# Reordering the first and the last steps of an attention stage: k's products first, first u's squares early, a copy of u later

## The chip, the cores and the metric

The kernel runs on one core of one Trainium2 chip. The metric is the device time of one execution in microseconds (us). It has five engines that matter here: TensorE (PE) for products, VectorE (DVE) and ScalarE (ACT) for element-wise work and for emptying PSUM, GpSimd (POOL) for small sums, and SyncE (SP), which only issues DMA transfers. ACT issues some transfers too. Each engine works through its own instructions in order and waits for the others by semaphores.

## The reference

The input x has 2 sequences of 2048 rows of 256 numbers, all in 32-bit floats. Four parts are added to x in turn, each on layer-normalised rows:

```python
x = x + attn_a(layernorm(x))   # gated scan: q * scan(a, kv)
x = x + ffn(layernorm(x))      # 256 -> 1024 -> 256, ternary weights, gelu
x = x + attn_b(layernorm(x))   # 16 heads of 64, below
x = x + ffn(layernorm(x))      # the same weights again
```

The third is the part that the change touches. With q, k and v from x by three 256 x 1024 matrices, each head carries three 64 x 64 states through time, and the result goes through W_o:

```python
k_C = k_t @ C_QV                  # then, per head:
G    = G    + outer(k_t, k_C)
S_K  = S_K  + outer(k_t, k_t)
C_QV = C_QV + outer(q_t, v_t)
o_t  = q_t @ (S_K @ C_QV - G)
```

## The kernel before

The program has three stages. The first does the gated scan and the first ffn (to about 310 us), the second the attention with states (310 to about 1040 us, overlapped with the first block of the last ffn), the third the rest of the last ffn.

The attention works in chunks of 128 rows. There are 32 steps `s`; step `s` is chunk `n = s // 2` of sequence `s % 2`, so that an even step (`first`) and the odd step after it form a pair. The states are rewritten as running sums: u is q times the running sum S of k's outer products, with a masked part inside the chunk, and o is q times the running sum M of outer products of u and v, built in the same way. The helpers for a step are these:

- `Seven` (L732) makes one of q, k, v for the two chunks of a pair with seven products instead of eight. `go` (L784) takes their numbers. Product 2 goes to bank Y and 1 to bank X; 0 stands for the addition of Y by DVE; 5 goes to bank Z; 6 and 7 go on top of X, 3 on top of Z, 4 on top of X again. Products 1, 5, 6 and 4 are followed by a copy out of their bank by ACT (L791, L796, L799, L808), products 7 and 3 by an addition on DVE (L782). Since 6, 7 and 4 write on the bank that the step before still has to be read from, each waits for the copy or the addition ahead of it. The tag (`uT`, `oT`) says from which two of the PSUM banks X and Z come; Y comes from a ring of four.
- `keys_out` (L946) and `units_out` (L949) turn a chunk of k or u into the other layout: DVE transposes squares of 32 x 32 (L923), SP writes them to DRAM (L925). `turn_rows` (L928) reads them back with four gathers on SP's queue (L933) into one of two buffers `raw`. `turn_end` (L939) and `units_end` (L952) copy the result on ACT (L943, to kT or uN).
- `inter` (L839) and `intra` (L855) make u or o from the state and from within the chunk, `products` (L823) the masked products q by k or q by u (DVE applies the mask at L837), `evict` (L869) empties the two banks of u or o in three copies (L873, L875), `update` (L878) adds to a state: S from k and k, M from u (uN) and v.
- `units` (L956) is the last step's way to uN: PE transposes and DVE copies (L818).
- `Last` (L1139) works the first block of the last ffn into the last steps: `part` issues blocks of 256 KB of its weights on ACT's DMA queue (L348), `begin` and `fill` (L1186, L1194) do its products (hx, hy, hz at L394).

The order of the work on PE, DVE, ACT and POOL is written by hand: it is the order of the calls. SP's transfers follow the same order. L964 to L985 open the stage, before the loop over the steps; the loop is L986 to L1109. What matters in it: at L1012 an even step copies the last step's u (`units_end(s - 1)`) ahead of its own work inside the chunk, and so does the last pair's odd step; the other odd steps do it at L1043, behind the evictions. An even step puts its own u out only at L1077 and reads it back at L1096.

Of the kernel before, what the change touches and what calls it, by code (L numbers as in the profile page):

```python
# [43 lines left out]
def kernel(  # L44
# [662 lines left out]
    def attention(keep, pool, state, last):  # L707
# [161 lines left out]
        def evict(s, nm, copy=act):  # L869
            b, n = steps[s]  # L870
            banks = d[s][nm + "b"]
            t = pool.tile([P, NPR, P], FP, tag=nm, bufs=2 if nm == "uT" else 1, name=f"{nm}{b}_{n}")
            copy(t[:, :, halves[0]], banks[0])  # L873
            for h in range(2):
                copy(t[halves[h], :, halves[1]], banks[1][halves[h ^ 1], :, :])  # L875
            d[s][nm] = t

        def update(s, left, right, sums):  # L878


            b, n = steps[s]
            prev = before.get((b, sums))
            last = n == CPB - 1
            banks = [bank([P, NPR, DK], f"h{sums}{b}_{n}_{c}") for c in range(1 if last else 2)]
            for p in range(NPR):
                for c in range(len(banks)):
                    for h in range(2):
                        nc.tensor.matmul(  # L888
                            banks[c][halves[h], p, :], lhsT=d[s][left][halves[c], feats(h, p)],
                            rhs=d[s][right][halves[c], feats(h, p)], start=True, stop=True,  # L890
                        )
            d[s][sums] = [prev]
            for c in range(len(banks)):
                t = state.tile([P, NPR, DK], FP, tag=f"{sums}{b}", bufs=3, name=f"{sums}{b}_{n}_{c}")
                if prev is None:
                    nc.vector.tensor_copy(t, banks[c])
                else:
                    nc.vector.tensor_tensor(t, prev, banks[c], ALU.add)  # L898
                d[s][sums].append(t)
                prev = t  # L900
            before[b, sums] = prev
# [26 lines left out]
        def turn_rows(s, nm):  # L928

            b, n = steps[s]  # L930
            raw = pool.tile([P, P, NPR], FP, tag="raw", bufs=2, name=f"r{nm}{b}_{n}")
            for b_ in range(NQ):
                nc.sync.dma_start(  # L933
                    out=raw[b_ * SQ : (b_ + 1) * SQ].rearrange("i (a j) q -> i a (j q)", a=NQ),
                    in_=d[s]["d" + nm][:, :, b_, :].rearrange("a i c -> i a c"),
                )
            d[s]["r" + nm] = raw

        def turn_end(s, nm):  # L939

            b, n = steps[s]
            t = pool.tile([P, NPR, P], FP, tag=nm, bufs=1, name=f"{nm}{b}_{n}")
            act(t, d[s]["r" + nm].rearrange("p t q -> p q t"))  # L943
            d[s][nm] = t

        def keys_out(s):  # L946
            turn_squares(s, "kT", d[s]["kN"].rearrange("t (q b i) -> t b q i", q=NPR, b=NQ))
# [8 lines left out]
        def units(s):  # L956
            uT = d[s]["uT"]
            turned(lambda p: uT[:, p, :], s, "uN", "raw")
            d[s]["uN"] = d[s]["uN"].rearrange("p a e -> p (a e)")
# [4 lines left out]
        NS = len(steps)  # L964
        pair_sums(0)
        stats = norm_stats(norm_pool, pair(1), bias=True)
        k, q = Seven(0, "kN", "uT"), Seven(0, "qT", "oT")
        k.go(2, 1)
        q.go(2, 1)
        k.go(0, 5, 6)  # L970
        q.go(0, 5, 6)
        xn = norm_rows(norm_pool, pair(1), stats)
        k.go(7, 3)
        keys_out(0)
        turn_rows(0, "kT")
        q.go(7)
        k.go(4)
        q.go(3, 4)
        v = Seven(0, "vN", "oT")
        v.go(2, 1)  # L980
        v.go(0, 5, 6)
        update(0, "kN", "kN", "S")
        v.go(7, 3)
        keys_out(1)
        turn_end(0, "kT")  # L985
        for s in range(NS):  # L986
            first, n = s % 2 == 0, s // 2
            more = n + 1 < CPB
            inter(s, "S", "uT")
            products(s, "kT", "p1")  # L990
            if first and n + 2 < CPB:
                stats = norm_stats(norm_pool, pair(n + 2), bias=True)
            elif s == NS - 4:
                last.stats()
            elif s == NS - 2:
                last.second_stats()
            if s == 0:
                v.go(4)
                pairs[1] = norm_turned(norm_pool, pair(1), xn, bufs=1)
                pair_sums(1)  # L1000
            if s % 2 == 1 and more:
                q, v = Seven(n + 1, "qT", "uT"), Seven(n + 1, "vN", "oT")
            if s == 1:
                q.go(2)
                v.go(2)
                keys_out(s + 1)
            elif s % 2 == 1 and s + 1 < NS:
                keys_out(s + 1)
            if s == 2:
                k = Seven(n + 1, "kN", "uT")  # L1010
                k.go(2)
            if s > 0 and (first or not more):  # L1012
                units_end(s - 1)
            last.part()
            if s >= 3:
                outward(s - 3, 1)
            intra(s, "S", "kN", "p1", "uT")
            if s >= 2:
                intra(s - 2, "M", "vN", "p2", "oT")
            if s + 1 < NS:  # L1020
                turn_rows(s + 1, "kT")
            evict(s, "uT")
            if not more:
                if s >= 2:
                    evict(s - 2, "oT")
                last.begin(first)
                fill = last.fill
                fill(2)
                if not first:
                    units(s)  # L1030
                fill(2)
            elif first:
                if s != 2:
                    k = Seven(n + 1, "kN", "uT")
                    k.go(2)
                k.go(1)
                if s >= 2:
                    evict(s - 2, "oT")
                k.go(0, 5)
            else:  # L1040
                if s >= 2:
                    evict(s - 2, "oT", dve)
                units_end(s - 1)  # L1043
                units_out(s)
                turn_rows(s, "uN")
                if s > 1:
                    q.go(2)
                    v.go(2)
                q.go(1)
                v.go(1)  # L1050
                q.go(0, 5)
                v.go(0, 5)
                q.go(6)
                v.go(6)
            last.part()
            if s == NS - 1:
                last.second_rows()
            if s + 1 < NS:
                update(s + 1, "kN", "kN", "S")
            if s >= 1:  # L1060
                update(s - 1, "uN", "vN", "M")
            if s == NS - 1:
                update(s, "uN", "vN", "M")
            if first and not more:
                turn_end(s + 1, "kT")
            if not more:
                fill(2)
            elif first:
                k.go(6, 3, 7)
            else:  # L1070
                v.go(7)
                q.go(7)
                v.go(3, 4)
                q.go(3)
            last.part()
            if first:
                units_out(s)  # L1077
            if more:
                turn_end(s + 1, "kT")
            if s >= 1:  # L1080
                inter(s - 1, "M", "oT")
                products(s - 1, "uT", "p2")
            if not more:
                fill(1)
            elif first:
                k.go(4)
                if n + 2 < CPB:
                    xn = norm_rows(norm_pool, pair(n + 2), stats)
                else:
                    last.rows()  # L1090
            else:
                q.go(4)
            if not first and s + 2 < NS:
                keys_out(s + 2)
            if first:
                turn_rows(s, "uN")  # L1096
            if not first and n + 2 < CPB:
                pairs[n + 2] = norm_turned(norm_pool, pair(n + 2), xn, bufs=1)
                pair_sums(n + 2)
            elif s == NS - 3:  # L1100
                last.turned()
            if s == NS - 4:
                last.weights(True)
            elif s == NS - 3:
                last.part(None)
                last.weights(False)
            last.part()
            if s >= 2:
                outward(s - 2, 0)  # L1109
# [17 lines left out]
    def pair(n):  # L1127
        return [b * CPB + n for b in range(B)]
# [96 lines left out]
    with tc.tile_pool(name="keep", bufs=3) as keep_pool:  # L1225
# [10 lines left out]
        with tc.tile_pool(name="ffn2", bufs=1) as ffn_pool, tc.manual_schedule(engines=by_hand):  # L1236
            tags = ("uT", "ps", "oT")
            steps = last.outs
            for i, g0 in enumerate(blocks):
                more = i + 1 < len(blocks)  # L1240
# [57 lines left out]
```

## Time and profile before

| | us |
|---|---|
| three runs, median (lowest to highest) | 1240.7 (1238.59 to 1245.66) |
| profiled execution, whole | 1239.59 |
| profiled execution, span | 1237.8 |
| PE busy | 1217.9 (98%) |
| DVE busy | 753.2 (61%) |
| ACT busy | 588.0 (48%) |
| PE busy in 350 to 360 us | 4.91 of 10 |
| PE busy in 500 to 900 us | 399.17 of 400 |
| PE busy in 1000 to 1020 us | 17.17 of 20 |
| mean granted PE clock | 0.999 |

The span runs from the first to the last instruction of the profiled execution; its whole time is 1.8 us more. A line of a profile names the engine, the line of the kernel, the tile written and the tiles read (hqT_X is bank X of q's products, hkN of k's, hvN of v's; huT, hoT, hS, hM and hp are the banks of u, o, S, M and the masked products), the shape and the count. In a list of waits it says who waited for whom, the total, the times and the longest.

### The profile page before, as it was taken

What the parts mean: (1) busy time and instruction counts of PE and PEld (TensorE: products, weight loads), DVE (VectorE), ACT (ScalarE), POOL (GpSimd) and SP (SyncE); (2) the same over time, 40 slices, a digit from 0 to 9 for tenths busy, and PEclk for the clock granted to TensorE, in tenths of its full rate; (3) what the DMA queues carried; (4) which work ended last, traced back from release to release, by engine and by line L of the source; (5) the groups of instructions that cost most, each with busy time, mean ns of one, the idle gap of its engine ahead of it and who ended that gap; (6) DMA issues with size and microseconds to landing.
All of it is one profiled execution on the core that took longest, in us unless ns stands there. A gap on an engine that the chain in (4) does not pass through costs nothing.

```text
span 1237.8 us, 46471 instructions
## 1 busy us (share of the span) xinstructions
PE 1217.9 (98%) x21244; PEld 976.1 (79%) x21244; DVE 753.2 (61%) x1261; ACT 588.0 (48%) x960; POOL 217.9 (18%) x363
## 2 busy tenths in 40 slices
PE   9999999999989999999999999999999989999998
PEld 7588777999557787777777778777777879999998
DVE  7965664665456565566557666665666644566654
ACT  4355544543445445444454544545454553445442
POOL 3743143322101100110110010011011100322230
PEclk9999999999999999999999999999999999999999
DMA  9210000000232233233233223323322530000001
GB/s 325 105 60 1 1 1 1 1 2 1 70 104 89 88 122 108 69 116 111 76 101 105 97 86 122 106 81 105 105 93 83 177 110 11 30 22 18 18 18 34
DMA packets 60995, 91.98 MB, mean 74 GB/s; under 512 B 6112, under 2 KB 49376, under 8 KB 60544
## 3 DMA queue, kind: packets, MB, share of 16 engines
q1 hardware_dynamic: 58272, 84.96, 20.4%
q10 hardware_dynamic: 2448, 3.93, 1.1%
q8 instruction: 166, 2.72, 0.9%
q0 software_dynamic: 80, 0.14, 0.1%
q14 instruction: 29, 0.24, 0.1%
HBM read 48.11 MB, written 40.89 MB: 72 GB/s over the span
## 4 chain that ended last, share of the span: by engine, by line
PE 95%; DMA 2%; DVE 1%; ACT 1%; issue 1%; SPq 0%; POOL 0%; ACTq 0%; DVEq 0%; POOLq 0%
PE ox L485 9%; PE hy L909 9%; PE hx L394 9%; PE pq L272 6%; PE hkN_X L777 5%; PE hqT_X L772 5%; PE hp L831 5%; PE oz L485 5%; PE hvN_X L777 4%; PE hz L394 4%; PE hoT L848 3%; PE hS L888 3%; PE huT L862 3%; PE huT L848 3%; PE hM L888 2%; PE hoT L862 2%
## 5 line engine op out<-in xcount | busy, mean ns | idle before, releaser
L837 DVE TENSOR_TENSOR p<-hp,mask 128x512 f32<-128x512 f32 x128 | 82.1, 683 | 99.2 <-PE hp L831 99.2
L909 PE MATMUL hy<-wo,oT 128*128 128x256 f32 x512 | 123.6, 385 | 0.0
L909 PEld LDWEIGHTS hy<-wo,oT 128*128 128x128 f32 x512 | 93.6, 190 | 18.9 <-issue 6.7
L729 POOL TENSOR_TENSOR S<-xnT 128x128 f32<-128x128 f32 x32 | 14.8, 461 | 527.4 <-ACT xnT L205 509.7
L406 ACT ACTIVATE hT<-hT,b_sb 128x256 f32<-128x256 f32 x192 | 85.4, 500 | 32.8 <-DVE hT L438 31.3
L272 PE MATMUL pq<-xnT,wqkva 128*128 128x512 f32 (+1 forms) x216 | 84.8, 547 | 0.3 <-ACT xnT L216 0.3
L873 ACT COPY uT<-huT 128x512 f32<-128x512 f32 x32 | 18.8, 586 | 136.8 <-PE huT L862 136.8
L898 DVE TENSOR_TENSOR S<-S,hS 128x512 f32<-128x512 f32 x60 | 41.3, 688 | 58.9 <-PE hS L888 55.4
L188 ACT ACTIVATE xn<-x_sb,nb,rs 128x256 f32<-128x256 f32 x124 | 64.7, 592 | 16.4 <-POOL nb L174 16.4
L943 ACT COPY uN<-ruN 128x1024 f32<-128x1024 f32 x31 | 64.4, 2078 | 14.1 <-DMA ruN<-duN 12.5
L272 PEld LDWEIGHTS pq<-xnT,wqkva 128*128 128x128 f32 x216 | 40.0, 190 | 37.3 <-issue 34.7
L943 ACT COPY kT<-rkT 128x1024 f32<-128x1024 f32 x32 | 66.6, 2081 | 2.6 <-DMA rkT<-dkT 2.6
L923 DVE STREAM_TRANSPOSE skT<-kN 128x1024 f32<-128x1024 f32 x32 | 65.6, 2050 | 0.0
L491 DVE TENSOR_TENSOR x_sb<-x_sb,ox 128x256 f32<-128x256 f32 x64 | 26.8, 418 | 63.0 <-PE ox L485 63.0
L923 DVE STREAM_TRANSPOSE suN<-uT 128x1024 f32<-128x1024 f32 x31 | 63.6, 2050 | 2.0 <-ACT uT L875 1.6
L412 ACT COPY hT<-hx 128x512 f32<-128x512 f32 x32 | 18.8, 586 | 91.3 <-PE hx L394 91.2
L156 DVE BATCH_NORM_STATS2 st<-x_sb 128x6 f32<-128x256 f32 x128 | 51.4, 402 | 2.9 <-DMA x_sb<-in_x_dram 2.4
L888 PEld LDWEIGHTS hS<-kN 64*64 64x64 f32 x1984 | 32.8, 134 | 24.2 <-issue 24.2
L371 POOL TENSOR_TENSOR xT<-xnT 128x256 f32<-128x256 f32 x15 | 10.9, 727 | 223.7 <-ACT xnT L218 223.7
L808 ACT COPY vN<-hvN_X 128x512 f32<-128x512 f32 x16 | 9.4, 587 | 80.0 <-PE hvN_X L777 80.0
L782 DVE TENSOR_TENSOR kN<-kN,hkN_Y 128x512 f32<-128x512 f32 x16 | 11.0, 688 | 57.0 <-ACT kN L791 57.0
L218 ACT COPY xnT<-pt 128x512 f32<-128x512 f32 x32 | 17.2, 589 | 58.5 <-PE pt L212 50.7
(243 smaller groups left out, 2915.0 us busy)
## 6 DMA issues: line engine op xcount, KB each, us to landing
dkT<-skT SPq DMA_DIRECT2D x32, 512.0 KB, 3.3
rkT<-dkT SPq DMA_DIRECT2D x128, 128.0 KB, 2.9
duN<-suN SPq DMA_DIRECT2D x31, 512.0 KB, 3.4
ruN<-duN SPq DMA_DIRECT2D x124, 128.0 KB, 3.1
out_dram<-x_sb SPq DMA_DIRECT2D x16, 256.0 KB, 2.1
x_sb<-in_x_dram SPq DMA_DIRECT2D x7, 512.0 KB, 8.9
dw<-w SPq DMA_DIRECT2D x2, 1024.0 KB, 3.9
w_back<-dw ACTq DMA_DIRECT2D x8, 256.0 KB, 4.5
```

The lines of the kernel that those rows point to most:

```text
L188: nc.scalar.activation(xn[:, c, :], x_sb[:, g, :], AF.Identity, bias=nb[:, c : c + 1], scale=rs[:, c : c + 1],)
L272: nc.tensor.matmul(pq[:, :nt], lhsT=wqkva[:, d, col : col + P], rhs=xnT[:, d, :], start=(d == 0), stop=(d == ND - 1),)
L394: nc.tensor.matmul(at[a][:, j, :], lhsT=A[:, f * P : (f + 1) * P], rhs=Bm, start=(new and j == 0), stop=True, skip_group_check=True,)
L406: nc.scalar.activation(out, out if src is None else src[:, j, :], AF.Gelu, bias=b1_sb[:, f : f + 1])
L485: nc.tensor.matmul(banks[name][:, c, :], lhsT=A[f // 2][:, f % 2, c * P : (c + 1) * P], rhs=Bm[:, f, :], start=(new and c == 0 and f == 0) ...
L777: nc.tensor.matmul(to, lhsT=self.A[i], rhs=self.B[i], start=new, stop=True, skip_group_check=True)
L837: nc.vector.tensor_tensor(d[s][nm][:, h], banks[h], mask8, ALU.mult)
L848: nc.tensor.matmul(banks[c][halves[h ^ c], p, :], lhsT=d[s][sums][c][halves[h], p, :], rhs=d[s]["qT"][halves[h], p, halves[c]], start=(p = ...
L888: nc.tensor.matmul(banks[c][halves[h], p, :], lhsT=d[s][left][halves[c], feats(h, p)], rhs=d[s][right][halves[c], feats(h, p)], start=True ...
L909: nc.tensor.matmul(py, lhsT=d[s]["oT"][:, p, :], rhs=wo[:, p, :], start=(p == 0), stop=(p == NPR - 1),)
L923: nc.vector.transpose(sq.rearrange("p b j q -> p b q j"), src)
L943: act(t, d[s]["r" + nm].rearrange("p t q -> p q t"))
```

## The change

Four things are done; the arithmetic stays the same.

1. At the opening of the stage k takes its banks from `oT` and q from `uT` (before the other way round). k's products come earlier than before among q's, and v's first ones are mixed in among the last ones of k and q. `keys_out(0)` with its gathers follows k's product 3, `keys_out(1)` k's product 4; before, the second stood at the end of the opening. v's product 6 now comes after `update`, right ahead of 7, and `turn_end(0)` moves ahead of v's 7 and 3.
2. In step 0, u goes out and is read back as soon as it is evicted (`units_out`, `turn_rows` behind k's product 1) instead of at the end of the step, and k's products 6, 3, 7 become 6, 7, 3.
3. In step 1, the copy of step 0's u moves from before step 1's own squares to behind the products 6 of q and v.
4. In the last step (31), the copy of step 30's u moves from before the work inside the chunk to behind the first two ffn products (the `fill(2)` at L1028), just ahead of `units`.

```diff
@@ -964,25 +964,29 @@
         NS = len(steps)
         pair_sums(0)
         stats = norm_stats(norm_pool, pair(1), bias=True)
-        k, q = Seven(0, "kN", "uT"), Seven(0, "qT", "oT")
-        k.go(2, 1)
-        q.go(2, 1)
-        k.go(0, 5, 6)
+        k, q, v = Seven(0, "kN", "oT"), Seven(0, "qT", "uT"), Seven(0, "vN", "oT")
+        k.go(2, 1, 0, 5)
+        q.go(2)
+        k.go(6)
+        q.go(1)
+        k.go(3)
+        keys_out(0)
+        turn_rows(0, "kT")
+        k.go(7)
         q.go(0, 5, 6)
         xn = norm_rows(norm_pool, pair(1), stats)
-        k.go(7, 3)
-        keys_out(0)
-        turn_rows(0, "kT")
+        v.go(2)
+        k.go(4)
+        keys_out(1)
         q.go(7)
-        k.go(4)
-        q.go(3, 4)
-        v = Seven(0, "vN", "oT")
-        v.go(2, 1)
-        v.go(0, 5, 6)
+        v.go(1)
+        q.go(3)
+        v.go(0, 5)
+        q.go(4)
         update(0, "kN", "kN", "S")
+        v.go(6)
+        turn_end(0, "kT")
         v.go(7, 3)
-        keys_out(1)
-        turn_end(0, "kT")
         for s in range(NS):
             first, n = s % 2 == 0, s // 2
             more = n + 1 < CPB
@@ -1009,7 +1013,7 @@
             if s == 2:
                 k = Seven(n + 1, "kN", "uT")
                 k.go(2)
-            if s > 0 and (first or not more):
+            if first and s > 0:
                 units_end(s - 1)
             last.part()
             if s >= 3:
@@ -1027,6 +1031,7 @@
                 fill = last.fill
                 fill(2)
                 if not first:
+                    units_end(s - 1)
                     units(s)
                 fill(2)
             elif first:
@@ -1036,11 +1041,14 @@
                 k.go(1)
                 if s >= 2:
                     evict(s - 2, "oT")
+                else:
+                    units_out(s)
+                    turn_rows(s, "uN")
                 k.go(0, 5)
             else:
                 if s >= 2:
                     evict(s - 2, "oT", dve)
-                units_end(s - 1)
+                    units_end(s - 1)
                 units_out(s)
                 turn_rows(s, "uN")
                 if s > 1:
@@ -1052,6 +1060,8 @@
                 v.go(0, 5)
                 q.go(6)
                 v.go(6)
+                if s == 1:
+                    units_end(s - 1)
             last.part()
             if s == NS - 1:
                 last.second_rows()
@@ -1066,14 +1076,14 @@
             if not more:
                 fill(2)
             elif first:
-                k.go(6, 3, 7)
+                k.go(*((6, 3, 7) if s > 0 else (6, 7, 3)))
             else:
                 v.go(7)
                 q.go(7)
                 v.go(3, 4)
                 q.go(3)
             last.part()
-            if first:
+            if first and s > 0:
                 units_out(s)
             if more:
                 turn_end(s + 1, "kT")
@@ -1092,7 +1102,7 @@
                 q.go(4)
             if not first and s + 2 < NS:
                 keys_out(s + 2)
-            if first:
+            if first and s > 0:
                 turn_rows(s, "uN")
             if not first and n + 2 < CPB:
                 pairs[n + 2] = norm_turned(norm_pool, pair(n + 2), xn, bufs=1)
```

## The prediction

> **What bounds the kernel now.** First the page of the kernel before: its engine totals, then its slices.
>
> ```profile
> span 1237.8 us, 46471 instructions
> ...
> PE 1217.9 (98%) x21244; PEld 976.1 (79%) x21244; DVE 753.2 (61%) x1261; ACT 588.0 (48%) x960; POOL 217.9 (18%) x363
> ...
> PE   9999999999989999999999999999999989999998
> ```
>
> TensorE (PE) sets the time; the change neither adds nor removes one of its instructions, so only its idle time can move. A slice is 30.9 us. The row dips in the 12th (340 to 371 us), the 33rd (990 to 1021 us) and the last, which the change doesn't touch. Between the first two there is nothing to win: by the windows, PE is busy 399.17 of the 400 us from 500 to 900. So I asked next for the stretches around the dips (columns after the engines: granted PE clock, DMA share, GB/s), and for PE's waits, once for 295 to 400 us and once for 960 to 1070 us (total, times, longest).
>
> ```profile
> 340.00:350.00 10.00, 9.22 (x202) 5.62 (x194) 7.53 (x8) 4.11 (x5) 0.00 (x0) 1.00 0.14 54
> 350.00:360.00 10.00, 4.91 (x36) 3.46 (x29) 3.46 (x4) 5.29 (x8) 0.00 (x0) 0.93 0.56 190
> 360.00:370.00 10.00, 10.00 (x194) 7.08 (x196) 5.43 (x9) 3.36 (x5) 0.00 (x0) 0.90 0.36 77
> ```
> ```profile
> PE hqT_X L772 <- ACT qT L791: 4.4, 1, 4.4
> ...
> PE hp L831 <- ACT kT L943: 1.2, 1, 1.2
> PE hqT_X L772 <- DVE qT L782: 0.8, 1, 0.8
> PE hkN_X L777 <- DVE kN L782: 0.8, 1, 0.8
> PE hqT_X L772 <- ACT uT L873: 0.7, 1, 0.7
> ```
> ```profile
> PE hx L394 <- ACT uT L873: 2.3, 1, 2.3
> PE hx L394 <- ACT hT L412: 0.4, 1, 0.4
> ```
>
> The reader is to see that a few single waits make up the whole dip, and that the clock falls below 1 only after the longest. Who holds PE is in ScalarE's (ACT) order of time, at the start and at the end (start, duration, then in brackets the idle time before):
>
> ```profile
> 356.46 2.02 ACT L943 COPY uN<-ruN 128x1024 f32<-128x1024 f32 x1 [4.49 <-DMA ruN<-duN]
> 358.39 0.58 ACT L791 COPY qT<-hqT_X 128x512 f32<-128x512 f32 x1
> ...
> 1012.75 2.02 ACT L943 COPY uN<-ruN 128x1024 f32<-128x1024 f32 x1 [7.63 <-DMA ruN<-duN]
> 1014.68 0.58 ACT L873 COPY uT<-huT 128x512 f32<-128x512 f32 x1
> ```
> ```profile
> 359.02 2.08 PE L772 MATMUL hqT_X<-S,wq_t 128*128 128x128 f32 x8 [4.42 <-ACT qT L791]
> 360.89 1.54 PE L777 MATMUL hvN_X<-wv_t,S 128*128 128x512 f32 x2
> 362.36 1.16 PE L888 MATMUL hS<-kN 64*64 64x64 f32 x64
> ...
> 1019.98 2.08 PE L888 MATMUL hM<-vN,uN 64*64 64x64 f32 x64
> ```
>
> Both times the copy of u's rows (uN) waits for its gather, and small evictions that PE needs are queued behind it.
>
> **The start, part by part.** I walk PE's new order with durations of the trace: 0.86 us for a product of k or v, 0.89 for one of q, 1.09 for a group of 64 x 64 products, 0.59 for an ACT eviction (0.04 after PE's end), 0.69 for a DVE add, 2.05 for a transposition on DVE or a turning copy on ACT. All starts at 310.09.
>
> *The opening products.* k's product 3 now ends at 316.2 instead of 318.8, so key squares go out on DVE at 316.9 instead of 319.65. Its write goes out at 319.15, and with the old 2.65 us to the reads and 5.7 more to landing, ACT's copy of kT runs from 327.5 to 329.6. PE wants it at about 330.7: the 1.2 us wait goes. The 0.8 us wait (q's product 4 behind a transposition on DVE) goes too: q's add ends at 323.8 and PE comes at 324.0. That is a thin 0.2 us, as is k's product 4 (add ends 319.5, PE comes 319.7). POOL's sums were ready at 310.70 to 312.06, ahead of every use. A new wait appears: v's product 6 is followed directly by 7 in the same bank, where update S stood between them, so PE waits out the eviction, 0.04 + 0.59 + 0.05 = 0.68. Sum: 0.81 + 1.21 - 0.68 = 1.34 us won.
>
> *Step 0.* The order 6, 7, 3 takes away the 0.78 us wait of product 4 (3's 0.86 now covers the add of 7) and puts the same 0.68 between 6 and 7: 0.10 won. u's squares stand on DVE ahead of k's first add, which runs some 1.2 us later than it would; update S's copies come after it and end near 340.4, 3 us before PE reads them, so nothing is paid. Without that cover it would be those 1.2. The write and four gathers of u leave SP's queue before the next keys' instead of behind them: the write at about 338.8 instead of 345.9, and even with its slow 5.0 us to the gathers and 5.5 to landing the rows are there by 349.3.
>
> *Step 1.* The 0.67 us wait at q's product 1 stays (uT's eviction is unchanged), so it starts at 350.83 - 1.44 = 349.39; q's product 6 follows after the next three at 353.0 instead of 359.02. The 4.42 goes, and the slow clock after it: from 359.02 to 362.36 two products took 3.34 us for 1.75, so 1.6. Then v's 6 ends at 354.8, update S runs to 355.9, and update M needs uN. Its copy stands on ACT behind v's eviction: 354.9 + 0.5 = 355.4 to 357.45. PE waits about 1.55, and M starts at 357.45 instead of 363.34. **Start: 1.34 + 0.10 + 4.42 + 1.6 - 1.55 = 5.9 us.** Queued behind this copy are v's last eviction, the next kT copy and q's last; the product that feeds the first of them ends only at 362.3, so all have over 4 us. The next gather of u needs the buffer this copy reads; it is released at 357.5, lands at some 362.5, and is wanted at about 367.
>
> Does the clock dip all the same? The trace shows full clock from 320 to 350 us through waits of 0.8, 1.2 and 0.8. [...] After the change there are four waits of 0.7 to 1.6 within 33 us. By the row the cost is 0[...]. I take the row, since its waits are nearest in size and place.
>
> **The end.** ACT no longer waits for the gather ahead of uT's eviction: that starts when the u products end, 1011.0, and with the six of uT and oT and the copy of hx (seven at about 0.6) ACT is at 1015.2. uN's copy is then 1015.1 to 1017.2; the rows had landed at 1012.7. On PE, hx starts at 1013.0 right after hy, the transposes end at 1015.0, hz at 1015.95, the second hx at 1017.0; M waits 0.2, starts at 1017.2 and takes 1.1 (its second half needs DVE's copies, done by 1017.1). The product behind it then starts at 1018.3 instead of 1021.99: **3.7 us**, made of the 2.3, the 0.4 and about 1 inside M's 2.08, less 0.2.
>
> One DMA moves: the second block of w_t_back (256 KB, on ACT's queue) stood behind the waiting copy at 1012.77 and now follows the first at about 1005, beside u's write and gather. [...] At the 400 GB/s of a lone keys' write here (0.66 us for 256 KB) that makes the rows 0.7 late. The row nearest, the two writes issued close together at 352.80 and 354.08, waited 4.9 us where one alone took 2.65: 2.2 late. The copy has 2.4 to spare, so both give 0; I take 0, with 0 to 1 in the range. It can't win anything either: the block is first used at 1040.
>
> **Sum.** 5.9 + 3.7 = 9.6 us. The profiled execution took 1239.59 (span 1237.8): 1230.0. The median of the three runs lies 1.1 above it, and would give 1231.1. I predict 1230.6, half way, 0.8% less.
>
> **Rivals.** *A, the wait moves.* The slacks of 0.2 us on DVE and 1.1 at kT fail, with keys' second write now right behind the first gather, and M waits longer. For it: a keys' write beside another doubled. Against: u's gather of 352.27 landed in 4.17 with two writes issued during it, the first keys' in 4.27 alone. Costs 2 to 4: 1232.6 to 1234.6.
>
> *B, the end gains little.* The moved block delays u's rows past 1015.1. With 3 us more than the slack, the end gives 0.7: 1233.6.
>
> *C, it does not do what it says:* the later stages take the shift back, so the time stays near 1240. Against it: PE is over 99% busy after 400 us, and all later queues shift together.
>
> *D, slower.* [...] each dip 1.6 us, as priced. It decides from six dips on (9.6 / 1.6), that is with the clock below 0.8 over much of the first 60 us of attention; eight lose 12.8: 1230.6 + 12.8 = 1243.4. Against: full clock through the waits of 320 to 350 us, and between the four waits lie 6 to 13 us of unbroken work.
>
> **How the numbers follow.** Forecast 0.73 (own range 1227.5 to 1234), A 0.13, B 0.06, C 0.05, D 0.03. A measurement of this kernel tells about 0.5%, 6.2 us, from no change: the limit is 1234.5. Faster: the forecast, three quarters of A, and B in good part, less its tail above 1234.5: 0.84. Same: 0.12. Slower: 0.04. The range's low end has no new waits at all (0.68 + 0.68 + 1.55 = 2.9 more, 1227) and half a microsecond of spread; the high end takes in A and B: 1226.5 to 1236.
>
> **What would show it.** In the profile after: no wait of hqT_X for qT's L791 beyond 1 us; hM waiting some 1.5 for uN at about 357; hvN_X and hkN_X each waiting 0.7 for their evictions; clock 1.00 in all windows of the start; hp without a wait for kT; hx without one for uT near 1013, and M there in 1.1. The gain at 364 us (first product behind M) near 5.9, the rest near 1018. It is wrong if the sums at these two points differ by over 2 us, if the clock dips again, or if waits turn up between 400 and 980 us.

## The result

The changed kernel takes 1232.82 us (median of 6 runs, 1231.81 to 1233.69) against 1241.22 (6 runs, 1237.67 to 1245.66) of the kernel before beside it: a ratio of 0.9931, interval 0.9908 to 0.9953, or 8.4 us less. Its profiled execution took 1232.83 (span 1231.1). The forecast was 1230.6.

The page of the changed kernel, totals and slices:

```profile
span 1231.1 us, 46475 instructions
...
PE 1215.9 (99%) x21244; PEld 974.6 (79%) x21244; DVE 752.6 (61%) x1261; ACT 588.3 (48%) x960; POOL 217.8 (18%) x363
...
PE   9999999999989999999999999999999999999998
```

The dip in the 33rd slice is gone, that in the 12th remains as an 8. The windows at the start (columns as before: span, engines, granted clock, DMA share, GB/s):

```profile
340.00:350.00 10.00, 8.56 (x179) 5.36 (x179) 5.30 (x6) 4.95 (x7) 0.00 (x0) 1.00 0.31 94
350.00:360.00 10.00, 8.47 (x161) 6.08 (x161) 5.32 (x7) 6.37 (x9) 0.00 (x0) 1.00 0.51 172
360.00:370.00 10.00, 9.76 (x259) 8.04 (x257) 6.92 (x9) 5.65 (x5) 1.76 (x4) 1.00 0.19 50
```

From 350 to 360 us PE is busy 8.47 instead of 4.91, at full clock. PE's waits of the changed kernel from 295 to 400 us, then from 955 to 1070 (total, times, longest):

```profile
PE hM L888 <- ACT uN L943: 1.5, 1, 1.5
...
PE hkN_X L777 <- ACT kN L799: 0.8, 1, 0.8
PE hvN_X L777 <- ACT vN L799: 0.7, 1, 0.7
PE hqT_X L772 <- ACT uT L873: 0.7, 1, 0.7
```
```profile
PE hM L888 <- ACT uN L943: 0.8, 1, 0.8
```

The wait of q's product 6 for its eviction (4.4), that of hp for kT (1.2) and those of hx (2.3 and 0.4) are gone; update M now waits for the copy of u's rows, at the start and at the end. ACT's order shows why. The copy no longer waits for its gather (no idle time stands before it), and it comes behind the evictions that PE needs:

```profile
355.33 0.59 ACT L799 COPY vN<-hvN_X 128x512 f32<-128x512 f32 x1 [0.27 <-PE hvN_X L777]
355.82 2.05 ACT L943 COPY uN<-ruN 128x1024 f32<-128x1024 f32 x1
...
1010.62 0.59 ACT L412 COPY hT<-hx 128x512 f32<-128x512 f32 x1
1011.10 2.06 ACT L943 COPY uN<-ruN 128x1024 f32<-128x1024 f32 x1
```

PE's products at the same places:

```profile
353.38 1.05 PE L772 MATMUL hqT_X<-S,wq_t 128*128 128x128 f32 x8
354.27 1.02 PE L777 MATMUL hvN_X<-wv_t,S 128*128 128x512 f32 x2
...
357.92 1.16 PE L888 MATMUL hM<-vN,uN 64*64 64x64 f32 x64 [1.53 <-ACT uN L943]
...
1013.21 2.08 PE L888 MATMUL hM<-vN,uN 64*64 64x64 f32 x64 [0.77 <-ACT uN L943]
```

To see where the time went I cut each execution at four products: **the start** runs from k's first product to step 1's update M (53.41 us before, 47.64 after), **the end** from the first ffn product hy of the last step to the product behind its update M (10.12 before, 7.38 after). That is 5.8 and 2.7, together 8.5. The two profiled executions are only 6.76 apart, because the front before the attention took 0.35 longer and the middle between the two places 1.4.

### The profile page after: what moved, and what is told of

Its sections match the earlier page's. It is cut to its first block, busy times and chain, and to the rows that moved or that the text cites. A ratio compares the mean times of both kernels' runs of the same rounds, so it can differ in the third digit from the quotient of the medians.

```text
span 1231.1 us, 46475 instructions
## 1 busy us (share of the span) xinstructions
PE 1215.9 (99%) x21244; PEld 974.6 (79%) x21244; DVE 752.6 (61%) x1261; ACT 588.3 (48%) x960; POOL 217.8 (18%) x363
## 4 chain that ended last, share of the span: by engine, by line
PE 96%; ACT 1%; DVE 1%; issue 1%; DMA 1%; POOL 0%; SPq 0%; ACTq 0%; DVEq 0%; POOLq 0%
PE hy L909 9%; PE ox L485 9%; PE hx L394 9%; PE pq L272 6%; PE hkN_X L777 5%; PE hp L831 5%; PE hqT_X L772 5%; PE oz L485 5%; PE hvN_X L777 5%; PE hz L394 4%; PE huT L862 3%; PE huT L848 3%; PE hoT L848 3%; PE hS L888 3%; PE hM L888 3%; PE hoT L862 2%
## 5 line engine op out<-in xcount | busy, mean ns | idle before, releaser
L477 DVE TENSOR_TENSOR hS<-hT 128x512 f32<-128x512 f32 x62 | 41.2, 686 | 5.6 <-ACT hT L406 5.6
```

## The experiments

All kernels in one table; "before" is the first profile of the kernel before. Start and end are cut as above; the waits are PE's longest single ones in them. Each ratio is to runs of the kernel before on the same chip, in three groups: 1239.14 (median of 50 runs, 1233.9 to 1243.87) for start_only, end_only, copy_late_only and copy_early, 1239.47 (55) for opening_only, squares_only, filled and best, 1240.48 (19) for the rest; after itself stands beside the 1241.22 above.

| kernel | median (range), us | ratio (interval) | start | end | waits |
|---|---|---|---|---|---|
| before | 1241.22 (1237.67–1245.66) | | 53.41 | 10.12 | 4.42, 2.31 |
| before_again | 1235.12, one run | | 48.33 | 11.44 | 1.63, 2.90 |
| after | 1232.82 (1231.81–1233.69) | 0.9931 (0.9908–0.9953) | 47.64 | 7.38 | 1.53, 0.77 |
| after_again | 1232.39 (1230.38–1232.88) | 0.9934 (0.9916–0.9952) | 47.64 | 7.37 | 1.53, 0.8 |
| start_only | 1236.66 (1233.24–1238.75) | 0.9981 (0.9967–0.9994) | 47.63 | 12.65 | 1.52, 2.95 |
| end_only | 1236.16 (1232.95–1239.47) | 0.9974 (0.9958–0.9989) | 48.32 | 7.37 | 1.64, 0.8 |
| opening_only | 1235.51 (1233.28–1240.78) | 0.9976 (0.9961–0.9990) | 52.20 | 10.58 | 4.47, 2.32 |
| squares_only | 1234.94 (1232.92–1237.80) | 0.9964 (0.9954–0.9975) | 46.74 | 10.49 | 0.8, 2.69 |
| copy_late_only | 1236.32 (1234.28–1238.61) | 0.9975 (0.9963–0.9987) | 48.13 | 10.10 | 1.53, 2.3 |
| copy_early | 1229.91 (1229.35–1232.95) | 0.9920 (0.9894–0.9945) | 46.19 | 7.36 | 0.8, 0.8 |
| filled | 1236.94 (1233.76–1240.53) | 0.9978 (0.9966–0.9990) | 52.75 | 10.38 | 2.74, 0.87 |
| filled_more | 1239.86 (1237.77–1242.91) | 0.9999 (0.9984–1.0014) | 52.00 | 11.35 | 1.1, 3.11 |
| best | 1229.27 (1227.78–1230.11) | 0.9913 (0.9893–0.9933) | 45.07 | 6.64 | 1.0, none over 0.6 |
| best_late | 1227.05 (1225.95–1227.94) | 0.9893 (0.9874–0.9912) | 45.82 | 6.64 | 0.3, none over 0.5 |

### The two halves

start_only is the changed kernel without edit 4, end_only the kernel before with edit 4 alone. The lines in question, as start_only has them against the changed kernel:

```diff
-            if first and s > 0:
+            if s > 0 and (first or not more):
                 units_end(s - 1)
...
                 if not first:
-                    units_end(s - 1)
                     units(s)
```

> The changed kernel with its fourth edit undone: the last step copies u where the kernel before does. Theory (the waits at the two places add up, and nothing between them matters): the first product behind update M of step 1 comes 5.6 us earlier than before, as in the changed kernel, and the end gives nothing, so the time is 8.4 - 2.7 = 5.7 us under the kernel before. Rival (the later stages take part of the start's gain back, as the 1.4 us lost between 364 and 968 us in the changed kernel's trace suggest): only about 4.2 us under it.

> The kernel before with the fourth edit alone. Theory: 2.7 us less than the kernel before, all of it between the last step's hy and the product behind update M; update M still takes 2.08 us there[...] and no wait is in it. Rival (my prediction's: about 1 us of the 2.08 was a wait for the second copy): 3.7 us less and update M in 1.1.

By place the halves are clean: start_only has the changed kernel's start (47.63), end_only its end (7.37). By the medians they are not: start_only is 2.5 us under the kernel before, where 5.7 was expected and 4.2 by the rival, end_only 3.0, where 2.7 was expected. That is 5.5 together, beside 8.1 and 8.4 for the whole change; only the upper ends of their intervals (0.7 to 4.1 us and 1.4 to 5.2) would make that up. And what each leaves alone is not what the first profile showed. The old end takes 12.65 in start_only instead of 10.12 (PE's products there):

```profile
1011.66 2.07 PE L394 MATMUL hx<-xnT,w_back 128*128 128x256 f32 x4 [2.95 <-ACT uT L873]
1013.52 1.91 PE L817 MATMUL huN<-ident,uT 128*128 128x128 f32 x8
1015.23 1.91 PE L394 MATMUL hz<-xT_last,w_s_back 128*128 128x256 f32 x4
1016.94 1.35 PE L394 MATMUL hx<-xT_last,w_s_back 128*128 128x256 f32 x4
```

After a wait of 2.95 these four took 6.56 us to update M, at a granted clock of 0.50 from 1012 to 1016 us; in the changed kernel the same four took about 3.6 at clock 1.00 (1008.82 to 1012.45). So the dip of the clock cost 3 us there, where the first profile of before, after a wait of 2.31, showed none (1.00 from 1010 to 1020 us). And the old start takes 48.32 in end_only instead of 53.41. So what part of the 53.41 is the code's and what the execution's?

### The same kernels once more

before_again is the unchanged kernel before, profiled a second time, after_again the changed one.

> The kernel before itself, for a second profiled execution. Theory (its time is spread by how late the gathers of u land and by the clock): the wait at q's product 6 of step 1 is between 1.6 and 4.5 us, that at hx near 1010 between 2.3 and 3.0, and what the clock does behind each may differ from the first execution. Rival (the waits are the same in every execution): 4.4 and 2.3 again, with clock 0.93 and 1.00 as then.

> The changed kernel once more, for a second profiled execution and more times. Theory (it has no PE wait over 1.6 us, so neither slow transfers nor the clock reach its time): a median within 0.5 us of 1232.8, a range under 3 us where the kernel before has 9 to 10, and clock 1.00 in both places. Rival (its narrow range was the chance of six runs): a range of 6 us or more.

The write of step 0's u and its gathers on SP's queue, in the first profile of the kernel before and then in the second:

```profile
345.91 0.34 SPq L925 DMA_DIRECT2D duN<-suN  x1
350.98 1.73 SPq L933 DMA_DIRECT2D ruN<-duN  x4
```
```profile
345.00 0.34 SPq L925 DMA_DIRECT2D duN<-suN  x1
348.34 1.73 SPq L933 DMA_DIRECT2D ruN<-duN  x4
```

The gathers wait for the write: 5.07 us in one execution, 3.34 in the other. The last of the four gathers then took 4.17 us to land in the first and 3.10 in the second: in the first execution, step 1's own write of u goes out (354.08) while it is under way, in the second (353.17) just after it has landed (352.73); that this is the cause is not shown. PE's product 6 of q waited 4.42 and 1.63, and only the first was followed by slow products (2.08 and 1.54 us; the clock from 360 to 370 us is 0.90 in the first, 1.00 in the second). In before_again:

```profile
355.33 1.16 PE L772 MATMUL hqT_X<-S,wq_t 128*128 128x128 f32 x8 [1.63 <-ACT qT L791]
...
1010.11 1.35 PE L394 MATMUL hx<-xnT,w_back 128*128 128x256 f32 x4 [2.90 <-ACT uT L873]
1011.30 1.97 PE L817 MATMUL huN<-ident,uT 128*128 128x128 f32 x8
```

The start differs by 5.1 us between two executions of one program: 2.8 by this wait (1.7 from the write, 1.1 from the gather), 1.4 by the slow products, 0.9 by the wait of hp for kT, which is not in every execution either: before and filled_more have it, before_again has not. Of the seven profiled executions that write u at its old place, the write took 4.6 to 5.2 us to the gathers in five (before, opening_only, copy_late_only, filled, filled_more) and 3.3 in two (before_again, end_only). Of the seven that write it early (from 337.3 to 339.4 us), it took 2.7 to 3.4 in all. The changed kernel's start and end repeat within 0.01 us.

### The start in its parts

opening_only is the kernel before with edit 1 alone, the first block of the diff above, complete; it begins

```diff
-        k, q = Seven(0, "kN", "uT"), Seven(0, "qT", "oT")
-        k.go(2, 1)
-        q.go(2, 1)
+        k, q, v = Seven(0, "kN", "oT"), Seven(0, "qT", "uT"), Seven(0, "vN", "oT")
+        k.go(2, 1, 0, 5)
+        q.go(2)
```

squares_only has edit 2 alone:

```diff
                     evict(s - 2, "oT")
+                else:
+                    units_out(s)
+                    turn_rows(s, "uN")
                 k.go(0, 5)
...
-                k.go(6, 3, 7)
+                k.go(*((6, 3, 7) if s > 0 else (6, 7, 3)))
...
-            if first:
+            if first and s > 0:
                 units_out(s)
...
-            if first:
+            if first and s > 0:
                 turn_rows(s, "uN")
```

copy_late_only has edit 3 alone, and copy_early is the changed kernel with edit 3 undone, as here:

```diff
-                    units_end(s - 1)
+                units_end(s - 1)
                 units_out(s)
...
-                if s == 1:
-                    units_end(s - 1)
```

> The kernel before with the new opening alone (first edit). Theory (what the profiled execution of before showed was partly chance: in end_only's trace, with the same opening, the products with kT waited only 0.1 us instead of 1.2): the opening removes 0.8 us of waiting behind the transposition and adds 0.7 behind v's product 6, so it gains 0.1 to 1.3 by how late the rows land, and the later waits are untouched: a median within 1.5 us of the kernel before, with as wide a range of times (some 8 us). Rival (my prediction's sum): 1.3 us less in every execution.

> The kernel before with the second edit alone: step 0's squares early, the copy in its old place. Theory (early squares alone remove the wait for the rows and the clock's fall behind it; they do not need the later copy): no wait of q's product 6 over 0.5 us at step 1, and the median comes 3 us or more under the kernel before, near copy_early less what the end and the opening give. Rival (the copy of u in ACT's order ahead of four evictions holds PE even when its rows are there): a wait of over 1.5 us at q's product 6, and no more than 1 us under it.

> The kernel before with the third edit alone: step 0's squares go out late as before, but its copy stands behind the products 6 of step 1. Theory (the two edits stand in for each other): the rows land at 356.4 as before, the copy runs from about 356.9 to 359, update M starts at 359 instead of 363.3 after a wait of about 1.7 us, short enough for full clock: 4.3 us under the kernel before. Rival (without early squares the wait only moves to update M and the clock falls there): update M at 361 or later and 2 us or less under it.

> The changed kernel with its third edit undone: step 1 copies step 0's u right behind the evictions of its own u again, while the squares still go out early. Theory (once the squares are early the rows are there in time, so the later copy is not needed and only puts update M behind it): the copy runs from 351 to 353, q's and v's evictions follow in time, update M starts about 356.3 instead of 357.9, and the time is 1.5 us under the changed kernel, some 9.9 under the kernel before. Rival (the copy ahead of four evictions holds q's product 6, as in the kernel before): PE waits over 1.5 us at that product and the time is that of the changed kernel or more.

opening_only had a slow write (5.20 us) like the first profile, and the same wait behind it (4.47 against 4.42); its start is 1.2 us shorter, for which 1.34 had been forecast. Its median, though, is 4.0 us under the kernel before, where at most 1.5 was expected. Its runs lie in two heaps, 12 from 1233.3 to 1235.9 and seven from 1237.1 to 1240.8, and the profiled one (1239.37) is of the upper heap; a quick write in more of its runs would do this, but no profile of the lower heap was taken, so it stays open. squares_only has no wait at q's product 6: 46.74, and its median is 4.5 us under, where 3 or more was expected. copy_late_only had a slow write too (4.87), yet its start is 48.13, since the copy comes when the rows are there and only M waits, 1.53; its median is 2.8 us under, not the 4.3 expected from the first profile. So edits 2 and 3 each do away with the wait, and they do not add up. With both, edit 3 costs. PE in copy_early:

```profile
353.61 1.16 PE L772 MATMUL hqT_X<-S,wq_t 128*128 128x128 f32 x8
...
356.54 1.11 PE L888 MATMUL hM<-vN,uN 64*64 64x64 f32 x64
```

Update M comes without a wait, 46.19 behind k's first product instead of 47.64: edit 3 costs 1.45 us once the squares go out early. The medians (1229.91 against 1232.82 and 1232.39) point the same way, and squares_only (edit 2 alone, 1234.94) lies under start_only (edits 1 to 3, 1236.66); but in both cases the intervals of the ratios overlap.

### Filling the wait

If the slow products come from PE standing still, work in the gap should save them. filled puts two extra products ahead of q's product 6 in step 1 and two between hy and hx of the last step of the kernel before; filled_more puts four at the first place and none at the second. Nothing reads what they write, so the output stays as it was.

```diff
+        def busy(times):
+            idle = bank([P, HK], "idle")
+            for _ in range(times):
+                nc.tensor.matmul(idle, lhsT=ident, rhs=wo[:, :2, :], start=True, stop=True)
...
-                fill(2)
+                fill(1)
+                if not first:
+                    busy(2)
+                fill(1)
...
                 v.go(0, 5)
+                if s == 1:
+                    busy(2)
                 q.go(6)
```

> The kernel before, all its waits kept, with two 128x512 products that nobody reads (1.7 us of PE time) put into each of the two long waits: ahead of q's product 6 in step 1, and between hy and hx of the last step. Theory (a good part of what the waits cost, and of the spread of the times of before, is the slow clock after an idle PE: 4 products at 1.9 instead of 0.9 us each in start_only's trace after 2.95 us of idle time): with at most 2.7 us idle in a row the clock stays at 1.00, the median falls by 1.5 to 3 us although work is added, and times above 1241 disappear. Rival (the spread is that of the transfers alone): the median is unchanged or higher and the range as wide as before.

> The kernel before with four unread products (3.4 us) ahead of q's product 6 in step 1 and none at the end. In filled, 2.7 us of idle time were left there and the clock still fell, so my bound of 2.7 was too high. Theory (the clock falls by the length of the idle stretch, with a border between 1.6 and 2.7 us): where the rows come as late as in filled, 1.0 us of idle time is left, the clock is 1.00 from 350 to 370 us, and q's and v's products 6 take 0.9 us each instead of 1.6 and 1.9; update M starts 1.5 us earlier than in filled. Rival (the slow clock comes from the burst of transfers at that time, not from idle time): clock under 0.95 there again.

PE in filled, then in filled_more:

```profile
358.82 1.76 PE L772 MATMUL hqT_X<-S,wq_t 128*128 128x128 f32 x8 [2.74 <-ACT qT L791]
360.37 1.91 PE L777 MATMUL hvN_X<-wv_t,S 128*128 128x512 f32 x2
```
```profile
359.35 1.16 PE L772 MATMUL hqT_X<-S,wq_t 128*128 128x128 f32 x8 [1.05 <-ACT qT L791]
360.34 1.02 PE L777 MATMUL hvN_X<-wv_t,S 128*128 128x512 f32 x2
```

With two products 2.74 of the wait are left and the clock dips all the same (0.96 from 350 to 360 us, 0.87 from 360 to 370); with four, 1.05 is left, the clock is 1.00 in both windows and both products have their usual length, behind an equally late u (the write took 4.59) and beside as many transfers (187 GB/s from 350 to 360 us, 190 in before). At filled's end the wait is 0.87 and the clock 1.00. The runs without a profile agree: the mean granted clock of each is on record, and its mean is 0.9974 over the 124 runs of the kernel before in the three groups, 0.9996 over the 22 of filled, and 0.9980 over the 12 of filled_more, whose end is not filled (wait 3.11, clock 0.84 from 1010 to 1020 us). So here the slow products went with the longer idle time, not with the transfers. As a remedy it is worth little: filled's median is 2.5 us lower, filled_more's is not (0.9999, interval 0.9984 to 1.0014). A likely reason, beside the end, is that in an execution with a quick write the wait is 1.6, less than the 3.4 that four products take. My expectation for filled, full clock with at most 2.7 us idle in a row, did not hold: the clock fell after 2.74.

### What is left over

best starts from the changed kernel: v's product 6 goes ahead of update S in the opening and k's 6 ahead of it in step 0 (so each eviction runs under the update), v's product 1 goes ahead of q's 1 in step 1, the last step's o is evicted by DVE instead of ACT, and edit 3 is undone. best_late keeps u's copy late instead, and puts products 7 of v and q ahead of update M. The core of best_late against the changed kernel:

```diff
-        update(0, "kN", "kN", "S")
         v.go(6)
+        update(0, "kN", "kN", "S")
...
-                    evict(s - 2, "oT")
+                    evict(s - 2, "oT", act if first else dve)
...
                 k.go(0, 5)
+                if s == 0:
+                    k.go(6)
...
+            if s == 1:
+                v.go(7)
+                q.go(7)
             if s >= 1:
                 update(s - 1, "uN", "vN", "M")
```

> The changed kernel with its own new waits taken out: v's product 6 ahead of update S in the opening, k's product 6 of step 0 ahead of update S too, the copy of u in step 1 back behind the evictions (third edit undone), v's product 1 ahead of q's there, and the last step's o evicted by DVE instead of ACT so that the copy of u comes 0.9 us earlier. Theory (each wait is worth what the trace shows for it, 0.7, 0.8, 1.5, 0.7 and 0.8): 4.4 us under the changed kernel, 1228.4, and 1.5 to 3 under copy_early. Rival (the waits hide one another, or the later stages take them back): no better than copy_early's 1229.9.

> best, with the copy of u in step 1 late again (third edit kept), and the products 7 of v and q moved ahead of update M of that step, so that 1.75 us of work stands in the wait of 1.5 us. Theory: no wait at q's product 6 (1.0 us in best) and none over 0.3 at update M: 0.7 to 1.0 us under best, 1228.4. Rival (DVE now has the two additions of products 7 ahead of M's copies, and something later waits for them): equal to best or slower.

PE's waits in best_late from 300 to 1070 us, and u's copy with the update that it feeds:

```profile
PE hkN_X L777 <- DVE kN L782: 0.3, 1, 0.3
PE huT L848 <- ACT qT L808: 0.2, 1, 0.2
```
```profile
353.23 2.07 ACT L943 COPY uN<-ruN 128x1024 f32<-128x1024 f32 x1
...
355.68 1.16 PE L888 MATMUL hM<-vN,uN 64*64 64x64 f32 x64
...
1007.20 2.08 PE L888 MATMUL hM<-vN,uN 64*64 64x64 f32 x64
```

These two are all of its waits on another engine; the others, up to 1.2 us, are put down to issue. The copy ends at 355.30, and M comes at 355.68 behind two products that were moved into the gap. best's median is only 0.6 us under copy_early's, where 1.5 to 3 was expected; product 6 of q waits 1.04 there behind u's copy. In best_late that wait is gone (its start of 45.82 holds those two products, 1.8 us, which best has behind M). best_late is the fastest kernel here: 1227.05, 13.4 us below the kernel before beside it and 5.3 below the changed one in the same group.

## Why the prediction was right, and where it was not

The direction, the places and the range held; the time is 2.2 us above the forecast. Step by step:

- **Opening, 1.34.** opening_only gives 1.2 against an execution with as slow a write. hp's wait for kT went as said (copy 328.21 to 330.26, PE at 331.04), though it is not in every execution of the kernel before. The two thin slacks held with 0.17 and 0.05 us left, and the new wait of v's product 7 is 0.67 (0.68 forecast).
- **Step 0, 0.10.** The new wait of k's product 7 is 0.77, not 0.68, and takes the place of one of 0.78: nothing won. The cover for DVE's squares held, and u's write went out at 338.88 (338.8 forecast).
- **Step 1, 4.42 + 1.6 − 1.55.** Right for this pair: no wait at q's product 6, no slow product, M waiting 1.53. The start gained 5.77 of the 5.9. (The slow clock's 1.6 is 1.4 if the same products of before_again are the measure.) But the pair is not the rule. Against before_again the same start gains 0.7. The step took one profiled execution's wait as the kernel's.
- **End, 3.7: mis-sized; it measured 2.74.** The failing term is "about 1 inside M's 2.08". I read the last update as one update of 64 products that waits half way. It is two, of steps 30 and 31, of 32 products each, because in a sequence's last chunk only the first half of the rows is used (L883), and the 2.08 is all work: in best_late and before_again nothing is left to wait for, and it is 2.08. DVE's two additions to M in the changed kernel stand 0.93 apart:

```profile
1014.41 0.69 DVE L898 TENSOR_TENSOR M<-M,hM 128x512 f32<-128x512 f32 x1 [0.69 <-PE hM L888]
1015.34 0.69 DVE L898 TENSOR_TENSOR M<-M,hM 128x512 f32<-128x512 f32 x1 [0.25 <-PE hM L888]
```

  The wait ahead of it is 0.77 where 0.2 was forecast, since PE came sooner: it took 4.6 us from hy to M's place in the line, not 5.1. That costs nothing by itself.
- **The moved weight block, 0.** Its two issues stand together near 1000.3. u's write took 4.05 us to the gathers (3.68 before), 0.37 more; that the block would make the rows late by its own 0.7 was my estimate. The copy started when ACT was free. Right.
- **The clock, 0.** 1.00 in every window of the start, through waits of 0.67, 0.77, 0.67 and 1.53, as through the 0.8, 1.2 and 0.8 of the kernel before. Rival D, repeated dips behind waits this short, had no trace for it and did not come up. Nor did A (kT was in time), B (the rows were there) or C: from 400 to 975 us no wait is longer than 0.5.
- **The sum.** 9.6 was forecast and 8.5 gained at the two places. The rest of the gap in this pair is the 1.8 us that front, middle and tail took more. That the change causes it is not shown: in after_again the middle is 2.4 us shorter than in after, with the same code. Over all profiled executions it lies between 641.9 and 645.8, counted from step 1's first product of o, from where all kernels have the same products; why is open.

**Why the median moved by 8.4 for all that.** In part by luck: the first profile of before (1239.59) lay near the median of its runs, so its waits stood in for the usual ones. Priced from before_again (1235.12), the two places would have given 0.7 and 4.1. The lowest of all runs of before is 1233.9, of the changed kernel 1230.4. That 3.5 is about what the code wins when nothing goes wrong, 0.7 at the start (48.33 to 47.64) and 2.7 at the end (10.1 to 7.4); it is a rough sign, since the one is the lowest of 130 runs and the other of 12. The highest are 1245.7 and 1233.7.

An estimate for the rest has two parts. The first is the slow clock. The mean granted clock is 0.9974 over the 124 runs of before and 0.9998 over the 12 of the changed kernel; of 1239 and 1232 us that is 3.2 and 0.3 us lost, 2.9 apart, if PE has work whenever the clock is low. Both places have a share in it: with only the start mended it is 0.9985 (squares_only), with only the end 0.9987 (end_only). The second is the longer wait at the start behind a slow write: 2.8 us, and the write is slow in five of the seven profiles that have it at its old place, so 2.0 on the mean. With the 3.4 that makes 8.3, beside medians 8.1 and 8.4 apart; hp's wait for kT and the waits above 2.3 at the end, some tenths, are left out. That the mean clock is lower in before is shown by its runs (down to 0.995, in the changed kernel to 0.999). That the write is slow as often without a profile is argued only, from the spread of the runs: 8 to 10 us for before, 2 to 3 for the changed kernel.

## To carry over

Profile the unchanged kernel twice before pricing a wait: a wait on a transfer just in time, and the slow clock behind it, can belong to one execution (here 4.42 us and clock 0.90, then 1.63 and 1.00), and a wide spread of the runs (here 8 to 10 us) is the sign of it. Where two edits attack one wait, price each with the other in place; the second may only cost. And before taking a long instruction group for a hidden wait, count the products and the rows that they use.

## What the hardware showed

**The clock fell after some long waits of PE, not after all.** After waits of up to 1.64 us (end_only) no product was slow. Between 2.3 and 3.1 us both happened: the clock fell after 2.32 (opening_only, 0.83 in a window of 10 us), 2.74 (filled, 0.87), 2.90 (before_again, 0.83), 2.95 (start_only, 0.50 from 1012 to 1016 us) and 3.11 (filled_more, 0.84), and stayed at 1.00 after 2.31 (before), 2.3 (copy_late_only) and 2.69 (squares_only). After 4.4 it fell both times (before to 0.90, opening_only to 0.89). The dip at the start cost 1.4 to 1.6 us, the longest at the end 3. Why equal waits ended differently is not shown.

**Few rows took as long as many.** In the changed kernel the last update M, 64 products of 64 x 64 that use one half of the rows, took 2.02 us to the next product, so 32 took about 1.0, as 64 products on both halves did (update M of step 1: 1.09 there, 1.04 in before_again). No run here varies the rows alone.

**A write ended late in some executions.** The DMA's busy share and GB/s from 344 to 352 us in slices of 0.2 us, in the first profile of before and then in before_again:

```profile
DMA  0000000000000397999900001000000000000001
GB/s 0 0 0 0 0 0 0 0 0 0 0 0 0 143 430 328 410 410 389 410 21 0 0 0 20 0 20 20 20 41 20 20 0 0 0 0 0 0 0 41
```
```profile
DMA  0000000008999995003000000002798887899999
GB/s 0 0 0 0 0 0 0 0 0 348 451 410 369 389 430 185 21 0 102 0 0 0 0 0 0 0 15 77 246 328 287 251 287 220 256 261 312 195 297 307
```

The bulk of u's 512 KB goes in 1.4 us both times. In the slow write single packets trail behind it until 350.4, and the gathers go out after them, at 350.98. In two of the other slow writes (filled, copy_late_only) the trail ends at 348.6, nothing is recorded for the next 1.9 us, and only then do the gathers go out; so trailing packets are not the whole cause. It stays open.
